# Identity transposes ahead of six matmul units of a perceiver block on one Trainium2 core

## The chip, the cores and the metric

The kernel runs on one core of a Trainium2 (trn2) chip. The metric is device time in microseconds (us) of one execution, the median of several runs. All data is float32.

## The reference

A block of a transformer over 32 sequences of 64 tokens, width 512, cut to what matters:

```python
x = x + cross_attention(layernorm(x), ctx, mask)   # 256 context tokens, one head, softmax
x = x + mla(layernorm(x))                          # 16 heads, low-rank q and kv, rope, causal
r = layernorm(x)                                   # FFN on 2048 tokens:
h = square(relu(r @ up_w))                         # 512 -> 2048
y = h @ down_w + (r @ expert_w) * top2(r @ gate_w).sum()
out = x + (layernorm(y) * gamma + beta)
```

## The kernel before

Only the last parts bear on the change. The kernel goes through five stages, one after the other on TensorE (PE): cross-attention and projections, the heads of the latent attention (b_q, b_s, b_t, b_v), the output projection ("op", matmuls into tiles op), the way up (tiles up) and the way down (tiles dp). The last three are matrix products of 2048 tokens, done as a scheme of seven block products in place of eight: a unit takes a left operand of 7 combined blocks and a right operand of 7, and writes seven products into four PSUM banks (`banks`, line 167: four tiles p0 to p3 of 128 x 2 x 256 float32, one bank each). Product s goes to half s % 2 of bank s // 2, so that the second half of bank 3 stays unused. Every operand is split into a high and a low part in fp32r (`split`, line 138: ACT's cast makes the high part, line 141; DVE's subtraction the low part, line 143), and every product is three matmuls: high by high, low by high, high by low (lines 699, 701, 702 in `seven`; line 1115 in `up_seven`, which has two blocks of the contraction and six matmuls a product).

The way up has 4 column blocks b by 8 weight slots k = 32 units of 42 matmuls, each 128x128 by 128x256. The weights wh_up and wl_up are the stationary operand there, the activations xr the moving one. In the first unit of each b (n = 0) four products go ahead with all but the last part of xr. After a unit `combine` (lines 154 to 162) adds the products on ACT and DVE, ACT squares (1183, 1184), and POOL adds the left blocks for the way down (`sums`, 149). Banks are double buffered (pool f_psp): a unit writes the banks of the last but one.

The way down has 8 token blocks by 8 slots = 64 units of 21 matmuls; the activations hl are stationary, the weights wh_down and wl_down moving. A token block accumulates its eight units in one set of banks. Units 0 to 15 alternate between the blocks 2 and 3 by fives and threes, then units 16, 24, 32, 40, 48 and 56 each begin a block. For every unit SP loads a tile c or dcw, POOL adds its missing blocks where they weren't stored (tokens of the first and the last column block), and ACT and DVE split it into hl (`left`), three units ahead of PE. After a block's last unit, `d_out` adds the experts' part (1260, 1262), normalizes (1269, 1270, 1285; the reciprocal root is POOL's power, line 121) and stores.

Before the way up, the last part of the projection stage turns the normalized tokens with transposes against the identity (line 959, tiles ops), and multiplies with the expert and gate weights (`o_expert`, tiles cpe; ACT scales into mo, lines 995 and 996, and issues the store itself, line 997). In the attention stage, b_t turns the softmax in groups of four transposes (line 779, tiles pst<-ident,s).

A recording layer (tc) orders the instructions of every engine by program order and its own estimate of readiness; `after(ins)` (line 135) pins what follows behind an instruction on its engine. Tiles come from pools at fixed places in SBUF; pools called gap shift what comes behind them. By those, the stationary and the moving operand of every fp32r matmul in the ways up and down lie at 32 and 96 bytes modulo 128 (wh_up 32, xr 96; hl 96, wh_down 32); the identity lies at 32.

Of the kernel before, what the change touches and what calls it, by code (L numbers as in the profile page):

```python
# [9 lines left out]
FP = mybir.dt.float32  # L10
# [8 lines left out]
P = 128  # L19
# [37 lines left out]

BETA_AT = 60

READ_AHEAD, READ_FAR = 5, 9  # L60

WARM = 10
# [17 lines left out]
def perceiver_block(ctx: ExitStack, tc: tile.TileContext, x, mem, mask, wq_a, bq_a, qnw, wq_b, bq_b,  # L80
                    wkv_a, bkv_a, kvnw, wkv_b, wo, bo, gate, up, down, expert, gamma, beta, cs, out):
    nc = tc.nc

    def pool(name, bufs=1, **kw):
        return tc.tile_pool(name=name, bufs=bufs, reuse_waits="tile", **kw)

    def gap(p, n, nm):

        p.tile([P, n // 4], FP, tag=f"gap_{nm}", name=f"gap_{nm}")
# [12 lines left out]
    cp = ctx.enter_context(pool("const"))  # L102
    mhalf = cp.tile([P, 2], FP, name="mhalf")
    nc.gpsimd.memset(mhalf, -0.5)
    pid = ExitStack()
    ident = pid.enter_context(pool("ident")).tile([P, P], FP, name="ident")
    make_identity(nc, ident)

    pows, stats_of, rooted = [], {}, {}
# [25 lines left out]
    def after(ins):  # L135
        return tc.issue_after(ins.ins) if ins is not None else ExitStack()
# [28 lines left out]
    def banks(pool, nm):  # L165

        return [pool.tile([P, 2, TB], FP, tag=f"p{i}", name=f"{nm}_{i}") for i in range(4)]
# [10 lines left out]
    with ExitStack() as mla:  # L178
# [409 lines left out]
        with ExitStack() as pb:  # L588
# [4 lines left out]
            one = pb.enter_context(pool("b_one"))  # L593
# [70 lines left out]
            cps, ops, reads = {}, {}, []  # L664
# [18 lines left out]
            def left(u, room=None, pins=(None, None)):  # L683
# [5 lines left out]
                ops[u] = (h, l)  # L689
                return low  # L690

            def seven(ps, k, h, l, steps=None, part=(0, 7)):

                wh, wl = wts[k]
                for s, (a, b) in list(enumerate(SEVEN))[slice(*part)]:
                    last = k == ORDER[-1] and s in (1, 3, 5, 6)

                    with after(first if k == 0 and s in (1, 3, 5) else None):
                        first = nc.tensor.matmul(  # L699
                            ps[s // 2][:, s % 2], h[:, a], wh[:, b], start=(k == 0 and s % 2 == 0), stop=False)  # L700
                    nc.tensor.matmul(ps[s // 2][:, s % 2], l[:, a], wh[:, b], start=False, stop=False)  # L701
                    ins = nc.tensor.matmul(ps[s // 2][:, s % 2], h[:, a], wl[:, b], start=False, stop=last)  # L702
                    if last and steps:
                        next(steps)
                return ins
# [116 lines left out]
            for j in range(n):  # L822
                g, blk = units[j]
# [47 lines left out]
            pss = {0: banks(ps_p, "op0")}  # L871
# [131 lines left out]
    for u, (blk, k) in enumerate(out_units):  # L1003
# [7 lines left out]
        if u >= 2:  # L1011
# [8 lines left out]
            o, steps = o_steps(blk, pss[blk]) if k == ORDER[-1] else (None, None)  # L1020
            seven(pss[blk], k, *ops.pop(u), steps)
        if u in SLOT_AT:
            i = 3 + SLOT_AT.index(u)
# [10 lines left out]
        if u in TURN_AT:  # L1034
            i = TURN_AT.index(u)
# [14 lines left out]
        if u in MULT_AT:  # L1050
            i = MULT_AT.index(u)
# [45 lines left out]
    for _ in o_expert(NB - 1, *xT):  # L1097
        pass
    pc.close()
    pid.close()  # L1100


    ps_p = ctx.enter_context(pool("f_psp", 2, space=PSUM))
    fp = ctx.enter_context(pool("f_act", 3))
    with ExitStack() as pu:
        gap(pu.enter_context(pool("gap4")), 192, "x")
        xps = [pu.enter_context(pool(f"u_x{i}")) for i in range(4)]

        def up_seven(ps, k, b, n, steps):
            wh, wl = (t[:, 0:7].rearrange("p a (k f) -> p a k f", k=2) for t in wts[k])  # L1110

            def product(s, parts, first=False, last=False):
                i, j = SEVEN[s]
                for m, (kk, w, low) in enumerate(parts):
                    nc.tensor.matmul(  # L1115
                        ps[s // 2][:, s % 2], w[:, i, kk], xr[b, 2 * kk + low][:, j],
                        start=(first and m == 0), stop=(last and m == len(parts) - 1),
                    )

            most = [(0, wh, 0), (0, wl, 0), (0, wh, 1), (1, wh, 0), (1, wl, 0)]  # L1120
            rest = [(1, wh, 1)]
            one, two = (0, 2, 4, 6), (1, 3, 5)
            late = None
            if n == 0:
                for s in one:
                    product(s, most, first=True)
            if n == 7:
                for s in one:
                    product(s, rest, first=True)
                for s in (0, 2, 4):  # L1130
                    product(s, most, last=True)
                for s in two:
                    product(s, rest, first=True)
                if b + 1 < NB // 2:
                    late = right(b + 1, 3)
            for s in range(7):
                if n == 0 and s in one:
                    product(s, rest, last=True)
                elif n < 7:
                    product(s, most + rest, True, True)  # L1140
                elif s in two or s == 6:
                    product(s, most, last=True)
                if s in (1, 3, 5, 6):
                    with after(late if s == 3 else None):
                        next(steps)
# [13 lines left out]
        for b in range(NB // 2):  # L1159
            if b == NB // 2 - 1:  # L1160
                first = [(blk, k) for ks in (ORDER[:5], ORDER[5:]) for blk in DOWN[:2] for k in ks]
# [3 lines left out]
            for n, k in enumerate(ORDER):  # L1165
# [11 lines left out]
                ps = banks(ps_p, f"up{b}_{k}")  # L1177
# [42 lines left out]
    with ExitStack() as pd:  # L1220
# [1 line left out]
        gab = wp.tile([P, D], FP, name="gab")  # L1222
        junk = wp.tile([P, D], FP, name="junk")
        sp = pd.enter_context(pool("d_small", 4))
        gap(pd.enter_context(pool("gap9")), 64, "hlq")
        hlq = pd.enter_context(pool("d_hl"))
        dcp = pd.enter_context(pool("d_c"))
        ap = pd.enter_context(pool("d_act", 2))
# [67 lines left out]
        def step(d, pins):  # L1296
            try:
                return d.send(pins)
            except StopIteration:
                return False  # L1300

        pss, xms, outs, read = {}, {}, [], 5
        for u, (blk, k) in enumerate(out_units):
            if k == ORDER[0]:
                pss[blk] = banks(ps_p, f"dp{blk}")
            while read <= min(max(u + READ_AHEAD, 2 * u + 1), u + READ_FAR, last_unit):
                read_pair(read, from_h, room_for(read))
                read += 1
            if u + 3 <= last_unit:
                room = hlq.tile([P, 7, TB], FR, tag="hl", name=f"hl{u + 3}") if u % 4 == 0 else None  # L1310
                low = left(u + 3, room=room)
            else:
                low = None, None
            o, steps = d_steps(blk, pss[blk]) if k == ORDER[-1] else (None, None)
            seven(pss[blk], k, *ops.pop(u), steps)
            if u in (8, 10) or (u > 15 and k == ORDER[4]):
                b = DOWN[(u - 8) // 2] if u < 16 else blk
                xms[b] = d_load(b)
            if u in (1, 4) and stores:
                store_h(*stores.pop(0))  # L1320
            if u == 6:
                nc.sync.dma_start(gab, gamma.partition_broadcast(P))
            if u in (1, 3, 5):
                put_slot(ORDER[5 + u // 2], "down", cs.pop(0))
            if u == 1:
                cs.append(read_slot(ORDER[7], "down"))
            outs = [d for d in outs if step(d, low)]
            if k == ORDER[-1]:
                outs.append(d_out(blk, o, *xms.pop(blk)))
                next(outs[-1])  # L1330
# [49 lines left out]
```

## Time and profile before

| what | value |
|---|---|
| runs | 1110.8, 1107.37, 1110.25 us; median 1110.25 |
| the profiled execution's own time | 1113.25 us |
| its span in the trace | 1111.5 us |
| mean granted TensorE clock | 0.989 |
| PE matmul busy | 1073.6 us, 97% |
| PE weight loads busy | 989.1 us, 89% |
| DVE, ACT, POOL busy | 773.3, 546.7, 509.3 us |
| way up, PE | from 781.19 to 939.8 us |
| way down, PE | from 940.56 to 1101.3 us |

How to read it: an execution is taken by the profiler, so its time stands beside the others, not among them. Busy time of PE is no measure of its pace, since matmuls overlap (one of 276 ns starts every 113 ns); the starts of matmuls in the timeline are. The granted clock is the share of full speed that the throttle let PE have. The chain of waits is followed back from the last instruction, at each step to what released it.

### The profile page before, as it was taken

Reading aid. Unit: us, or ns where it says so; the run is one execution under the profiler, and the core shown is the slowest. Engines: PE = TensorE matmul, PEld = TensorE weight load, DVE = VectorE, ACT = ScalarE, POOL = GpSimd, SP = SyncE. Lnnn points to the kernel's source line nnn. Section 1 sums busy time; section 2 is a strip of 40 time slices with the busy share of each in tenths; the row PEclk is TensorE's granted clock in tenths of the full one; section 3 lists DMA queues with packets and bytes.
Section 4 is the critical chain, followed back from the end, with each engine's and each line's share of the span. In section 5 each row is a group of like instructions: output and inputs, shape, how many; then the busy total and the mean of one; then the engine's idle time right before and its main releaser. Section 6 shows DMA issues by size and latency. Waiting matters only on the chain.

```text
span 1111.5 us, 25983 instructions
## 1 busy us (share of the span) xinstructions
PE 1073.6 (97%) x10182; PEld 989.1 (89%) x10182; DVE 773.3 (70%) x1363; ACT 546.7 (49%) x1048; POOL 509.3 (46%) x694
## 2 busy tenths in 40 slices
PE   8899999999999999999998999998999999999896
PEld 6677777689999999999888999998999999999896
DVE  4666666656766667666868866668776578698786
ACT  4444444433444434433555544445675667565543
POOL 3333333326778777774571200002058770056761
PEclk9999999999999999999999999999999999999998
DMA  8777666343686787773497776776766789998681
GB/s 266 224 230 234 212 209 207 110 159 125 252 276 212 249 273 274 257 244 109 146 367 277 254 229 229 218 284 239 239 190 201 236 290 280 307 314 253 188 247 58
DMA packets 195386, 254.67 MB, mean 229 GB/s; under 512 B 18544, under 2 KB 140032, under 8 KB 195264
## 3 DMA queue, kind: packets, MB, share of 16 engines
q1 hardware_dynamic: 190848, 241.45, 66.4%
q10 hardware_dynamic: 3456, 8.39, 2.1%
q0 software_dynamic: 960, 3.18, 0.8%
q8 instruction: 80, 1.31, 0.5%
q14 instruction: 42, 0.34, 0.1%
HBM read 146.67 MB, written 106.30 MB: 228 GB/s over the span
## 4 chain that ended last, share of the span: by engine, by line
PE 58%; DMA 13%; DVE 10%; POOL 6%; issue 5%; ACT 4%; SPq 2%; DVEq 0%; ACTq 0%; POOLq 0%
PE up L1115 9%; PE pss L749 6%; PE psq L173 4%; PE psq L174 4%; PE psq L175 4%; PE psv L793 3%; PE op L702 3%; PE op L701 3%; PE op L699 2%; DVE hl L143 2%; PE pse L173 2%; PE pse L175 2%; PE pse L174 2%; PE dp L701 2%; PE dp L702 2%
## 5 line engine op out<-in xcount | busy, mean ns | idle before, releaser
L731 DVE SCALAR_TENSOR_TENSOR qe<-pse,bqp,cq 64x256 f32<-64x256 f32 x256 | 123.7, 483 | 79.4 <-PE pse L175 73.5
L1115 PE MATMUL up<-xr,wh_up 128*128 128x256 f32 x896 | 156.7, 280 | 1.9 <-ACT up L154 1.9
L1115 PEld LDWEIGHTS up<-xr,wh_up 128*128 128x128 f32 x896 | 137.2, 190 | 2.3 <-ACT up L154 2.0
L701 PE MATMUL dp<-wh_down,hl 128*128 128x256 f32 x448 | 125.4, 280 | 4.2 <-DVE hl L143 4.2
L701 PE MATMUL op<-wh_wo,hl 128*128 128x256 f32 x448 | 125.9, 281 | 3.6 <-DVE hl L143 3.5
L143 DVE TENSOR_TENSOR hl<-c,hl 128x896 fp32r<-128x896 f32 x85 | 97.6, 1151 | 45.4 <-ACT hl L141 41.5
L699 PE MATMUL op<-wh_wo,hl 128*128 128x256 f32 x448 | 126.0, 282 | 1.8 <-ACT hl L141 1.8
L699 PE MATMUL dp<-wh_down,hl 128*128 128x256 f32 x448 | 125.2, 279 | 0.6 <-DVE uo L159 0.6
L702 PE MATMUL dp<-wl_down,hl 128*128 128x256 f32 x448 | 125.1, 279 | 0.0
L702 PE MATMUL op<-wl_wo,hl 128*128 128x256 f32 x448 | 124.9, 280 | 0.0
L1115 PE MATMUL up<-xr,wl_up 128*128 128x256 f32 x448 | 123.5, 279 | 0.0
L141 ACT CAST hl<-c 128x896 fp32r<-128x896 f32 x85 | 79.9, 941 | 80.7 <-PE op L702 33.1
L173 PE MATMUL psq<-qa_hi,qh 128*128 128x256 f32 x384 | 112.8, 294 | 0.0
L174 PE MATMUL psq<-qa_hi,ql 128*128 128x256 f32 x384 | 106.6, 278 | 0.0
L175 PE MATMUL psq<-qa_lo,qh 128*128 128x256 f32 x384 | 106.5, 277 | 0.0
L701 PEld LDWEIGHTS op<-wh_wo,hl 128*128 128x128 f32 x448 | 85.2, 190 | 5.1 <-DVE hl L143 5.0
L701 PEld LDWEIGHTS dp<-wh_down,hl 128*128 128x128 f32 x448 | 84.8, 189 | 4.6 <-DVE hl L143 4.6
L699 PEld LDWEIGHTS op<-wh_wo,hl 128*128 128x128 f32 x448 | 85.0, 190 | 2.7 <-ACT hl L141 2.0
L702 PEld LDWEIGHTS dp<-wl_down,hl 128*128 128x128 f32 x448 | 85.5, 191 | 0.0
L699 PEld LDWEIGHTS dp<-wh_down,hl 128*128 128x128 f32 x448 | 84.8, 189 | 0.7 <-issue 0.7
L702 PEld LDWEIGHTS op<-wl_wo,hl 128*128 128x128 f32 x448 | 84.8, 190 | 0.2 <-DVE wl_wo L143 0.2
L1115 PEld LDWEIGHTS up<-xr,wl_up 128*128 128x128 f32 x448 | 85.0, 190 | 0.0
(227 smaller groups left out, 3151.8 us busy)
## 6 DMA issues: line engine op xcount, KB each, us to landing
c<-vd SPq DMA_DIRECT2D x58, 448.0 KB, 4.2
cx<-in_ctx SPq DMA_DIRECT2D x32, 512.0 KB, 4.5
vd<-vw SPq DMA_DIRECT2D x29, 512.0 KB, 4.0
hd<-uo SPq DMA_DIRECT2D x107, 128.0 KB, 3.1
hd<-uw SPq DMA_DIRECT2D x21, 512.0 KB, 3.0
dcw<-hd SPq DMA_DIRECT2D x18, 448.0 KB, 5.5
vd<-v SPq DMA_DIRECT2D x30, 256.0 KB, 3.4
c<-hd SPq DMA_DIRECT2D x17, 448.0 KB, 6.2
```

Of the source, the lines that this page charges most:

```text
L141: copy = nc.scalar.copy(hi, src)
L143: return copy, engine.tensor_tensor(lo, src, hi.bitcast(FP), ALU.subtract)
L173: nc.tensor.matmul(ps, ah, bh, start=(j == 0), stop=False)
L174: nc.tensor.matmul(ps, al, bh, start=False, stop=False)
L175: nc.tensor.matmul(ps, ah, bl, start=False, stop=(j == n - 1))
L699: first = nc.tensor.matmul(ps[s // 2][:, s % 2], h[:, a], wh[:, b], start=(k == 0 and s % 2 == 0), stop=False)
L701: nc.tensor.matmul(ps[s // 2][:, s % 2], l[:, a], wh[:, b], start=False, stop=False)
L702: ins = nc.tensor.matmul(ps[s // 2][:, s % 2], h[:, a], wl[:, b], start=False, stop=last)
L731: rope = nc.vector.scalar_tensor_tensor(qe[64 * a : 64 * a + 64, :], pe[r, :], bqp[r, p : p + 1], cq[r, a, :], ALU.add, ALU.mult,)
L749: nc.tensor.matmul(ps[64 * j : 64 * j + 64, pj, b, :], qs[2 * pj + j][a][:, sl], kT[:, a, kt], start=(a == 0), stop=(a == 1),)
L793: nc.tensor.matmul(o, kv[a, i, :], t[a, bp, :], start=True, stop=True)
L1115: nc.tensor.matmul(ps[s // 2][:, s % 2], w[:, i, kk], xr[b, 2 * kk + low][:, j], start=(first and m == 0), stop=(last and m == len(parts) ...
```

## The change

Ahead of six units PE turns a 128x128 tile of the unit's stationary operand against an identity, twice, into the unused half of bank 3; nothing reads the result. The six are the first units of b = 0 and b = 2 of the way up, with wh_up against a second identity at 96 bytes modulo 128, which ACT copies from the first as the way up begins; and units 5, 16, 32 and 48 of the way down, with hl against the first identity, which now is kept to the end. Each tile turned lies 64 bytes from its identity modulo 128. The unit's matmuls are pinned behind the transposes (in the way up, those of its first four products), and in the way down the transposes behind the unit before. The second identity's place takes that of a gap ahead of the tiles of xr, and a gap in the way down grows, so that the other operands keep their places modulo 128.

```diff
--- before.py
+++ after.py
@@ -57,6 +57,8 @@
 
 BETA_AT = 60
 
+SETTLE_AT = (5, 16, 32, 48)
+
 READ_AHEAD, READ_FAR = 5, 9
 
 WARM = 10
@@ -102,8 +104,7 @@
     cp = ctx.enter_context(pool("const"))
     mhalf = cp.tile([P, 2], FP, name="mhalf")
     nc.gpsimd.memset(mhalf, -0.5)
-    pid = ExitStack()
-    ident = pid.enter_context(pool("ident")).tile([P, P], FP, name="ident")
+    ident = ctx.enter_context(pool("ident")).tile([P, P], FP, name="ident")
     make_identity(nc, ident)
 
     pows, stats_of, rooted = [], {}, {}
@@ -689,6 +690,13 @@
                 ops[u] = (h, l)
                 return low
 
+            def settle(ps, sta, one, behind):
+
+                for i in range(2):
+                    with after(behind):
+                        behind = nc.tensor.transpose(ps[3][:, 1, 0:P], sta.bitcast(FP), one)
+                return behind
+
             def seven(ps, k, h, l, steps=None, part=(0, 7)):
 
                 wh, wl = wts[k]
@@ -1097,13 +1105,14 @@
     for _ in o_expert(NB - 1, *xT):
         pass
     pc.close()
-    pid.close()
 
 
     ps_p = ctx.enter_context(pool("f_psp", 2, space=PSUM))
+    gap(ctx.enter_context(pool("gap11")), 192, "ident2")
+    ident2 = ctx.enter_context(pool("ident2")).tile([P, P], FP, name="ident2")
+    nc.scalar.copy(ident2, ident)
     fp = ctx.enter_context(pool("f_act", 3))
     with ExitStack() as pu:
-        gap(pu.enter_context(pool("gap4")), 192, "x")
         xps = [pu.enter_context(pool(f"u_x{i}")) for i in range(4)]
 
         def up_seven(ps, k, b, n, steps):
@@ -1122,8 +1131,9 @@
             one, two = (0, 2, 4, 6), (1, 3, 5)
             late = None
             if n == 0:
-                for s in one:
-                    product(s, most, first=True)
+                with after(settle(ps, wh[:, 0, 0], ident2, None) if b in (0, 2) else None):
+                    for s in one:
+                        product(s, most, first=True)
             if n == 7:
                 for s in one:
                     product(s, rest, first=True)
@@ -1222,7 +1232,7 @@
         gab = wp.tile([P, D], FP, name="gab")
         junk = wp.tile([P, D], FP, name="junk")
         sp = pd.enter_context(pool("d_small", 4))
-        gap(pd.enter_context(pool("gap9")), 64, "hlq")
+        gap(pd.enter_context(pool("gap9")), 128, "hlq")
         hlq = pd.enter_context(pool("d_hl"))
         dcp = pd.enter_context(pool("d_c"))
         ap = pd.enter_context(pool("d_act", 2))
@@ -1312,7 +1322,10 @@
             else:
                 low = None, None
             o, steps = d_steps(blk, pss[blk]) if k == ORDER[-1] else (None, None)
-            seven(pss[blk], k, *ops.pop(u), steps)
+            h, l = ops.pop(u)
+            even = settle(pss[blk], h[:, 0], ident, ends) if u in SETTLE_AT else None
+            with after(even):
+                ends = seven(pss[blk], k, h, l, steps)
             if u in (8, 10) or (u > 15 and k == ORDER[4]):
                 b = DOWN[(u - 8) // 2] if u < 16 else blk
                 xms[b] = d_load(b)
```

Lines 957 and up of the changed kernel are those of the kernel before moved by 8 to 13; `settle` is at lines 693 to 698, and line 1115 becomes 1124.

## Prediction

> **What bounds the kernel now.** I read four views, in this order: the table by stretches of time (which engine is full in the two ways), the chain that ended last, PE's timeline around waits and transposes, and ACT's timeline where the way up begins. All times are us from the start of the span.
>
> The chain first, from its list in order of time (start, us, what):
>
> ```profile
> 781.36 38.26 PE up L1115 x336
> 819.63 62.19 PE up L1115 x546
> 882.50 1.98 DVE xr L1086
> ...
> 1037.55 1.26 POOL dcw L149 x3
> ...
> 1041.83 1.27 DVE hl L143
> ```
>
> From 781 to 882 the chain is matmuls and nothing else: PE sets the time there. From 882.5 to 1043.1 it holds DMAs, DVE, ACT and POOL, and hardly a matmul: there PE waits for others (2.0 us at 921.3, 0.7 at 939.8, 1.4 at 955.0, 3.2 at 1039.9). After 1043.1 it is PE again up to the last matmul at 1101.3, and then the last block's DVE work.
>
> PE itself has two speeds at full clock. The same matmul, the group of line 701, taken in 941 to 1039 and in 1047 to 1101 (columns after the bar: busy us, mean ns of one):
>
> ```profile
> L701 PE MATMUL dp<-wh_down,hl 128*128 128x256 f32 x285 | 78.8, 276 | 1.2 <-DVE hl L143 1.2
> ```
>
> ```profile
> L701 PE MATMUL dp<-wh_down,hl 128*128 128x256 f32 x154 | 43.3, 281 | 0.0
> ```
>
> Of the difference the starts tell more: unit 20 of the way down starts at 989.82 and unit 21 at 992.20, so 21 matmuls take 2.380 us, 113.3 ns a step; units 50 and 51 start at 1066.80 and 1069.27, 2.473 us, 117.8 ns a step. Call them quick and slow. A unit of the way up (42 steps) is 4.760 or 4.947. The speed holds until PE is interrupted. In this execution up units 0 (first half) and 21 to 31 were slow, up units 1 to 20 quick, down units 0 to 40 quick, 42 to 63 slow.
>
> What transposes do to it, from PE's timeline (start, us):
>
> ```profile
> 545.72 0.28 PE L173 MATMUL pse<-qa_hi,qh 128*128 128x256 f32 x1
> 545.84 0.28 PE L174 MATMUL pse<-qa_hi,ql 128*128 128x256 f32 x1
> 545.96 0.28 PE L175 MATMUL pse<-qa_lo,qh 128*128 128x256 f32 x1
> 546.08 0.60 PE L779 MATMUL pst<-ident,s 128*128 128x128 f32 x4
> 546.43 0.37 PE L173 MATMUL psq<-qa_hi,qh 128*128 128x256 f32 x1
> ...
> 547.55 0.28 PE L173 MATMUL psq<-qa_hi,qh 128*128 128x256 f32 x1
> 547.66 0.28 PE L174 MATMUL psq<-qa_hi,ql 128*128 128x256 f32 x1
> ```
>
> Steps of 0.118 before, 0.113 after. Thirty such groups of four (tile and identity 64 bytes apart modulo 128, as in the change) stand in the attention stage: all were followed by quick steps, three of them after slow ones (257.6, 267.6, 546.1), as was the group at 559.7 that came after a wait.
>
> **The change part by part.** *Price of one pair.* From 545.96 to 547.55 is 1.59 us with four transposes and ten steps in it; ten quick steps are 1.13, so the four cost 0.46. They start 0.109 apart; two fewer leave 0.24 us a pair.
>
> *Pair ahead of up unit 0.* It does more than transpose: in the built order its first matmul waits for ACT's copy into ident2, which stands on ACT behind the last scaling of the experts (L996) and behind the issue of their store (L997):
>
> ```profile
> 781.82 0.49 ACT L996 ACTIVATE mo<-cpe,gs 128x256 f32<-128x256 f32 x1
> 782.34 0.33 ACTq L997 DMA_DIRECT2D mod<-mo  x1
> 784.63 0.37 ACT L154 COPY up<-up 128x256 f32<-128x256 f32 x1 [2.32 <-PE up L1115]
> ```
>
> ```profile
> 781.19 0.28 PE L1115 MATMUL up<-xr,wh_up 128*128 128x256 f32 x1
> ```
>
> Before, PE went straight on at 781.19. Now the issue ends at 782.67, the copy starts at about 782.70 and takes 0.27 (the 128x128 copy of line 492, median 270 ns), and PE follows 0.05 later (as after ACT's copy at 922.97): 783.02. The transposes start 0.165 and 0.109 apart after a wait (group at 559.7), and the first step after them takes 0.20, not 0.11: the unit runs as from 783.38 and ends at 788.14. Before it ended at 786.13, having lost 0.18 to slow steps and a 0.08 wait at 783.55 for xr's last part, which DVE has ready at 783.47, no longer late. **+2.01 us**, all on the chain: PE has nothing else queued, and behind it wait ACT's copy of line 154, DVE's and POOL's sums. Bounds: +0.06 if the copy were hidden (0.24 less 0.18), and +2.9 more if the clock drops (rival 2). I take 2.01, since it is read from the rows at the place itself.
>
> *Pair ahead of up unit 16* (857.84): it was quick already; **+0.24** on the chain. Its new wait, DVE's last sum of unit 14, is a unit old.
>
> *Pairs ahead of down units 5, 16, 32:* quick already. PE's waits at 955.0 (1.4) and 1039.9 (3.2) end with DVE's hl, not with PE, and cover 0.24 and 0.48: **0**; without the cover +0.72.
>
> *Pair ahead of down unit 48* (1061.85): 16 slow units turn quick, 16 x (2.473 - 2.380) = 1.49, less 0.24: **-1.25**. DVE's and ACT's parts of hl are there 2.2 us or more ahead of PE in units 48 to 63, so nothing is late next; the DVE end (1101.4 on) moves with the last matmul.
>
> *Moved rows:* in the built order DVE scales two output blocks (L1285, 1.03 us) ahead of hl37 and hl53 instead of behind, and ACT swaps their casts with a square; hl37 and hl53 had 2.2 and 3.0 us to spare: 0. POOL and SP keep their order. The new places of tiles keep the 64 byte relation. 0.
>
> Sum: 2.01 + 0.24 + 0 - 1.25 = **+1.0 us** on 1113.25, the profiled execution's time (span 1111.5): 1114.25. By the median of the runs, 1110.25/1113.25 = 0.9973: **1111.3 us**.
>
> *Rules against rows.* The Trainium skill, "TensorE: Matmul & The Clock Gate", Part 4: PE-mode transpose, says that the clock gate does not count transposes as PE activity as it does matmuls; by that the pair at up unit 0 would lengthen the idle time there and make rival 2 the forecast (+3.9). The rows say otherwise: 619.64 to 623.05, with eight transposes in it, kept the full clock. The same page, section Back-to-back issue gap, has one warm step, N/2.4 + 2.5 ns, an estimate of 109 ns here, and no second one; by it every pair is pure cost and the sum 2.01 + 0.24 + 0.24 = +2.5. The trace shows 113.3 and 117.8.
>
> **The rivals.** *1. The tail gains nothing* (the pair leaves slow steps slow, or the runs compared have a quick tail): 1.0 + 1.49 = +2.5, 1112.7. For it: no pair of two is in the trace, only fours and eights. Against: every group of four worked, and slow steps followed all four half-clock stretches, the one at 1042.9 among them.
>
> *2. The idle time before up unit 0 halves the clock.* The clock drops for 3.41 us at a time, the drops are whole multiples of 3.413 us apart, and what counts is the stretch just before (columns: length, PE busy, ..., PEclk):
>
> ```profile
> 619.64:623.05 3.41, 2.09 (x17) 1.68 (x15) 3.34 (x7) 2.40 (x4) 0.00 (x0) 1.00 0.67 222
> 623.05:626.47 3.42, 3.40 (x26) 3.20 (x27) 3.42 (x7) 1.04 (x2) 0.00 (x0) 1.00 0.69 189
> ...
> 920.01:923.42 3.41, 1.56 (x14) 1.39 (x13) 2.94 (x5) 3.32 (x6) 0.00 (x0) 1.00 0.76 284
> 923.42:926.84 3.42, 3.42 (x16) 3.42 (x17) 2.90 (x6) 2.88 (x5) 0.00 (x0) 0.50 0.89 243
> ```
>
> PE busy 1.56 (and 1.62 at 585.5) was too little, 2.09 enough. The new wait, 781.36 to 783.02, leaves 1.75 in a stretch that holds it whole, between the two; most positions of the stretch cut it in two and leave more. Price: steps of 213.3 instead of 113.3 ns for 3.41 us, 1.6; then slow steps, as after every such drop, for some seven units at 0.187, 1.3. In all +3.9, 1114.1: slower by 0.35%. It decides once the wait leaves less than about 1.6 busy; each 0.1 us of longer wait makes it likelier.
>
> *3. Slow steps of 882 to 940 matter after all* and the pair at unit 16 prevents them: 11 x 0.187 = 2.05 less, and 1.6 more if PE's wait at 921 then keeps the clock: -1.05 to -2.65, 1109.2 to 1107.6. Against: they began at 881.6 with a short wait, five units past that pair, and the chain leaves PE there.
>
> *4. The copy is early* (ACT's scaling ends sooner than PE's last expert matmul allows in this trace): 1.0 - 1.95 = -0.95; with rival 3, -3.0 to -4.6, 1105.7 at best. That would be faster by 0.4%.
>
> **How the numbers follow.** Forecast 0.50; rival 1 0.18; rival 2 0.18 (in a quarter of it with rival 1, 1115.6); rival 3 0.08; rival 4 0.06. The three runs spread over 3.4 us, two half-clock drops' worth, which blurs every case by about 1.7. 0.3%, 3.3 us, is about what a measurement of this kernel can tell from no change. Slower by more than that: rival 2 and some of rival 1, 0.23. Faster: rival 4 with 3 and spread, 0.07. The rest, 0.70, is within. The range, 1108.6 to 1114.8, takes in rivals 1 and 2 and the slower half of rival 3.
>
> **What would show it.** PE idle about 1.7 us before line 1124's first matmul, ended by ACT's copy; steps of 0.113 in all of up unit 0; no change of speed at unit 16; PE's waits at down units 6 and 41 shorter by the pairs' price; 2.380 us a unit from 48 on. I am wrong if PE starts the way up within 0.5 us, if the pair leaves slow steps, or if the waits between 882 and 1043 shrink by more than 0.7 us in all.

## The result, and the profile after

The kernel with the transposes takes **1114.53 us** (median of 10 runs, 1111.99 to 1116.74); the kernel before took 1111.65 us (10 runs, 1107.37 to 1113.06) timed beside it. The ratio is **1.0029, 95% interval 1.0015 to 1.0043**: slower by about 3.2 us, where +1.0 was forecast. The profiled execution, one of the ten, took 1115.56 us (span 1113.8, granted clock 0.992).

Where the time went is read from PE's starts, stage by stage. Each column is one execution; the second execution of each kernel ("again") was profiled later.

| from PE's starts, us | before | before, again | after | after, again |
|---|---|---|---|---|
| last expert matmul to first matmul of the way up | 0.12 | 0.12 | 1.74 | 1.74 |
| way up (first matmul to first of the way down) | 159.37 | 160.48 | 162.34 | 162.31 |
| way down (first matmul to last) | 160.75 | 157.11 | 158.28 | 158.98 |
| sum | 320.23 | 317.70 | 322.36 | 323.03 |
| half-clock stretches of 3.41 us in the two ways | 2 | 0 | 0 | 1 |

By the means the gap gives +1.62, the way up +2.4 and the way down -0.3: +3.7 us in all, beside the 3.2 (1.7 to 4.8) of the timed runs. So there are two things to explain: the gap, which was forecast, and a longer way up, which was not. The split by stage is rough. The half-clock stretches (923.4 and 1042.9 in before, 925.6 in after, again), at the 1.6 us each that the prediction worked out, are in the sums and differ by execution. And what lies ahead of the change varies more than the change costs: the last expert matmul starts between 778.2 and 785.1 us in the eighteen executions profiled, which is why sums and not spans are compared here.

**The gap.** PE's timeline in the profile after, where the way up begins (start, us, what; in brackets the idle time and what ended it):

```profile
781.24 0.28 PE L176 MATMUL cpe<-we_lo,oh 128*128 128x256 f32 x1
782.78 0.44 PE L697 MATMUL up<-ident,wh_up 128*128 128x128 f32 x2 [1.26 <-ACT ident L1113]
782.98 0.36 PE L1124 MATMUL up<-xr,wh_up 128*128 128x256 f32 x1
```

and ACT's there:

```profile
781.56 0.47 ACT L1004 ACTIVATE mo<-cpe,gs 128x256 f32<-128x256 f32 x1
782.06 0.33 ACTq L1005 DMA_DIRECT2D mod<-mo  x1
782.43 0.30 ACT L1113 COPY ident<-ident 128x128 f32<-128x128 f32 x1 [0.40 <-ACT mo L1004]
```

Scaling, issue of the store, copy, and 0.05 later PE: the chain is the one that the prediction drew. ACT's last scaling began 0.32 after the last expert matmul's start here, 0.74 in the profile before (781.08 to 781.82), where ACT's cast of xr had ended late; so the wait is 1.26, not 1.66.

**The clock.** The stretch of 3.41 us just before the way up (columns: length, PE busy, PEld, DVE, ACT, POOL busy, granted clock, DMA share, GB/s):

```profile
779.60:783.01 3.41, 2.15 (x20) 1.95 (x18) 2.59 (x4) 2.66 (x6) 0.00 (x0) 1.00 0.63 197
783.01:786.42 3.41, 3.41 (x31) 3.41 (x30) 0.63 (x1) 0.00 (x0) 0.00 (x0) 1.00 0.96 341
```

With 2.15 busy the next stretch has the full clock: no half-clock drop, as the forecast had it.

**The pace.** The durations of the same matmul show it at a glance: 276 ns among quick steps (113.3 ns from start to start), 281 among slow steps (117.8). From 787 to 877 (units 1 to 19 of the way up in the kernel before, 0 to 18 in the kernel after; min/median/max ns, first and last start); first the kernel before:

```profile
L1115 PE MATMUL up<-xr,wh_up x529: 276/276/356, 786.8 to 876.9; 128*128 128x256 f32 x177
```

then the kernel after:

```profile
L1124 PE MATMUL up<-xr,wh_up x510: 281/281/364, 786.9 to 876.9; 128*128 128x256 f32 x170
```

PE was quick there and is slow now, up to unit 28. In the second executions the kernel before was quick in units 0 to 20 again; the kernel after was slow to unit 15 and quick from 16 on, yet its way up was as long: PE then waited 3.1 us ahead of unit 29 (at 925.3), where the first execution had waited 1.3, and a half-clock stretch followed. In the way down, the same view of the low by high matmul (line 709) in units 8 to 15 and 17 to 40:

```profile
L709 PE MATMUL dp<-wh_down,hl x54: 276/276/276, 964.7 to 982.8; 128*128 128x256 f32 x54
...
L709 PE MATMUL dp<-wh_down,hl x155: 281/281/281, 985.1 to 1039.7; 128*128 128x256 f32 x155
```

Units 42 to 47 are quick again (median 276) after the wait at 1046.3, 49 to 63 slow again (281). The two changes from quick to slow stand exactly at the pairs of units 16 and 48. PE's timeline at unit 16:

```profile
983.79 0.28 PE L709 MATMUL dp<-wh_down,hl 128*128 128x256 f32 x1
983.90 0.28 PE L710 MATMUL dp<-wl_down,hl 128*128 128x256 f32 x1
984.01 0.38 PE L697 MATMUL dp<-ident,hl 128*128 128x128 f32 x2
984.15 0.36 PE L707 MATMUL dp<-wh_down,hl 128*128 128x256 f32 x1
984.35 0.28 PE L709 MATMUL dp<-wh_down,hl 128*128 128x256 f32 x1
984.47 0.28 PE L710 MATMUL dp<-wl_down,hl 128*128 128x256 f32 x1
```

Steps of 0.11 up to the pair, 0.12 after it. From 983.90 to 984.35 the pair costs 0.45 less two quick steps, 0.22 us (0.24 was forecast); what it leaves behind is the opposite of what was forecast.

### The profile page after: what moved, and what is told of

Its sections match the earlier page's. It is cut to its first block, busy times and chain, and to the rows that moved or that the text cites. A ratio compares the mean times of both kernels' runs of the same rounds, so it can differ in the third digit from the quotient of the medians.

```text
span 1113.8 us, 26008 instructions
## 1 busy us (share of the span) xinstructions
PE 1076.4 (97%) x10194; PEld 990.4 (89%) x10194; DVE 772.6 (69%) x1363; ACT 547.2 (49%) x1049; POOL 506.2 (45%) x694
## 4 chain that ended last, share of the span: by engine, by line
PE 27%; DMA 8%; DVE 7%; ACT 3%; issue 2%; POOL 2%; SPq 1%; DVEq 0%; ACTq 0%; POOLq 0%
PE up L1124 11%; PE op L710 2%; PE op L709 2%; PE op L707 2%; DVE hl L144 2%; PE dp L709 2%; PE dp L710 2%; PE dp L707 2%; DMA cw_wo<-wd_wo 2%; DMA c<-hd 1%; DMA cw_down<-wd_down 1%; PE cpe L175 1%; PE cpe L174 1%; PE cpe L176 1%; DMA dcw<-hd 1%
## 5 line engine op out<-in xcount | busy, mean ns | idle before, releaser
L1124 PEld LDWEIGHTS up<-xr,wh_up 128*128 128x128 f32 x896 | 137.5, 189 | 2.4 <-ACT up L155 1.5
```

What stands on the lines that cost most here:

```text
L1124: nc.tensor.matmul(ps[s // 2][:, s % 2], w[:, i, kk], xr[b, 2 * kk + low][:, j], start=(first and m == 0), stop=(last and m == len(parts) ...
```

## The experiments

Three accounts are tested. *The wait*: the cost is PE's wait for ACT's copy, and the pairs are worth next to nothing. *The slow pair*, in two forms that stood when the first four kernels were written: the pairs leave PE slow, because two transposes are too few, or because of the place of the tiles and weights that they stand ahead of. *The draw*, which came with the kernel counts: the pairs do not set a pace; every interruption of PE, a pair as well as a wait, lets it come out quick or slow, and the changed kernel loses by the slow stretches behind them. Beside these, whether the 64 bytes matter.

The table holds all executions with a profile. Times are from PE's starts as above (gap: last expert matmul to first matmul of the way up); the pace is that of the way up's units, q quick, s slow, without odd units behind the waits at its end; the ratio is to the kernel before, timed beside it, and stands where a kernel was timed in several runs. Half-clock stretches lie in the two ways of before (2), after_again (1), up0_pool (2), six (2) and apart (1).

| kernel | gap | way up | way down | sum | pace of the way up | ratio, 95% interval |
|---|---|---|---|---|---|---|
| before | 0.12 | 159.37 | 160.75 | 320.2 | 0-20 q, 21-31 s | |
| before_again | 0.12 | 160.48 | 157.11 | 317.7 | 0-20 q, 21-29 s | |
| after | 1.74 | 162.34 | 158.28 | 322.4 | 0-28 s | 1.0029 [1.0015, 1.0043] |
| after_again | 1.74 | 162.31 | 158.98 | 323.0 | 0-15 s, 16-31 q | |
| pool_copy | 0.25 | 158.29 | 159.75 | 318.3 | 0-20 q, 21-28 s | 1.0007 [0.9986, 1.0027] |
| up_only | 1.73 | 160.07 | 158.98 | 320.8 | 0-15 q, 16-31 s | 1.0024 [1.0009, 1.0039] |
| up_only_again | 1.73 | 163.12 | 157.21 | 322.1 | 0-28 s | |
| down_only | 0.12 | 161.96 | 156.84 | 318.9 | 0-28 s | 0.9992 [0.9976, 1.0009] |
| four | 1.95 | 159.59 | 157.69 | 319.2 | 0-15 q, 16-30 s | 1.0012 [0.9992, 1.0032] |
| up0_only | 1.73 | 162.81 | 159.31 | 323.9 | 0-31 s | 1.0066 [1.0047, 1.0086] |
| up0_again | 1.73 | 162.44 | 156.97 | 321.1 | 0-28 s | |
| up16_pool | 0.12 | 161.24 | 159.12 | 320.5 | 0-15 s, 16-30 q | 1.0013 [0.9996, 1.0030] |
| up0_pool | 0.26 | 156.66 | 160.07 | 317.0 | 0-26 q, 27-28 s, 29-31 q | 1.0009 [0.9995, 1.0023] |
| up0_pool_again | 0.26 | 158.88 | 157.28 | 316.4 | 0-30 q | |
| six | 0.72 | 159.62 | 161.39 | 321.7 | 0-30 q | 1.0026 [1.0007, 1.0045] |
| six_again | 0.69 | 162.18 | 158.50 | 321.4 | 0-29 s | |
| counts | 0.12 | 170.18 | 158.33 | 328.6 | 19 of 32 q | |
| apart | 0.12 | 167.17 | 161.20 | 328.5 | 8 of 32 q | |

### Which part costs: pool_copy, up_only, down_only, four

**pool_copy** takes the wait away: POOL, idle there, makes the copy.

```diff
-    nc.scalar.copy(ident2, ident)
+    nc.gpsimd.tensor_copy(ident2, ident)
```

> The copy into ident2 is moved from ACT to POOL, which is idle then; nothing else changes. Both theories (the pairs leave PE slow because two transposes are too few; or because of the place of the tiles and weights they stand ahead of) expect the same here: PE's gap ahead of up unit 0, 1.53 us in the changed kernel, falls to 0.3 (bank 3 is still released by ACT's scaling of the experts, at about 781.5), so 1.2 to 1.4 us less than the changed kernel, a ratio to the kernel before of about 1.0017, with up units 0 to 20 still slow at 4.947. A rival, that the late start is the whole loss, expects 1.0003 or less.

Measured 1.0007 [0.9986, 1.0027]; the gap is 0.25 us. The transposes are all still there, and most of the loss is gone (the intervals of 1.0029 and 1.0007 overlap, so this alone does not settle it). The ratio lies between the two that were expected, and units 0 to 20, expected slow, were quick: a pair does not always leave slow steps.

**up_only** keeps the pairs of the way up alone:

```diff
-SETTLE_AT = (5, 16, 32, 48)
+SETTLE_AT = ()
```

> The two pairs of the way up alone; the four of the way down are left out. If the slow way up is the loss (21 units on the chain at 0.187, 3.9 us, and 1.6 for the late start, part of which later waits of PE take back), the ratio to the kernel before stays at that of the changed kernel, about 1.0025 (1.0015 to 1.0035). If the pairs of the way down carry the loss, it falls to 1.0005 or less.

Measured 1.0024 [1.0009, 1.0039], the loss of the whole change, as expected if the way up carries it. But in the profiled execution units 0 to 15 were not slow, so the profile does not show the reason that the expectation gave.

**down_only** keeps those of the way down alone, without the copy:

```diff
-    nc.scalar.copy(ident2, ident)
...
-                with after(settle(ps, wh[:, 0, 0], ident2, None) if b in (0, 2) else None):
+                with after(None):
```

> The four pairs of the way down alone, no second identity is written. If the slow way up is the loss, the ratio to the kernel before is 1.000 within 0.0010: units 16 to 41 turn slow, which PE's wait at unit 41 (3.2 us in the kernel before) covers, and units 48 to 63 are slow either way. If the pairs of the way down carry the loss, it is 1.002 or more.

Measured 0.9992 [0.9976, 1.0009]: the pairs of the way down neither cost nor bring anything that can be measured. The expected pace did not come: units 5 to 31 were quick, 32 to 40 slow, 42 to 63 quick. And its way up, without a pair, was slow in units 0 to 28 (161.96 us): the unchanged stream of matmuls is not always quick, and a slow way up alone did not make this execution's sum, 318.9, longer than the mean of the two of before, 319.0, since its way down was quick to the end.

**four** has four transposes in place of two:

```diff
-                for i in range(2):
+                for i in range(4):
```

> Four transposes in place of two at all six places. Theory one, that two are too few (all groups of four or eight in both traces were followed by quick steps): up units from 0 on and down units from 5, 16, 32 and 48 on run at 4.760 and 2.380, the time falls by 3.9 in the way up and rises by 6 x 0.22 at most, ratio to the kernel before 1.000 to 1.001. Theory two, that the place counts (all six stand ahead of slot 0, whose weights lie 512 bytes modulo 1024 from those of the slots ahead of which the groups of eight stood): the same units stay slow, 4.947 and 2.473, ratio 1.003 to 1.004.

Measured 1.0012 [0.9992, 1.0032]. Of its six groups four were followed by quick steps; of the 18 pairs in the traces of after, pool_copy, up_only and down_only it was seven. So a pair does not reliably leave PE quick, which was the step that the forecast rested on; nor do four, and the place alone does not leave it slow. The ratio lies between the two that were expected and decides nothing.

### What decides the pace: counts and apart

**counts** puts 1, 2, 3, 4, 6 or 8 transposes ahead of every unit of the way up (by b: 2 and 4 by turns, 4 and 2, 1 and 3, 8 and 6), and 2, 4, 8, 2, 4, 8 ahead of six units of the way down, with POOL's copy (in the traces of counts and apart the groups of units 0 and 1 stand inside the units, not ahead of them):

```diff
-            def settle(ps, sta, one, behind):
+            def settle(ps, sta, one, behind, n=2):
-                for i in range(2):
+                for i in range(n):
...
+            with after(settle(ps, wh[:, 0, 0], ident2, past[0], ((2, 4) * 4, (4, 2) * 4, (1, 3) * 4, (8, 6) * 4)[b][n])):
```

> A probe of PE's pace: ahead of each of the 32 units of the way up stand 1, 2, 3, 4, 6 or 8 transposes (2 and 4 ten times each... in blocks 0 and 1 by turns 2,4 and 4,2; 1 and 3 in block 2; 8 and 6 in block 3), and ahead of six down units 2, 4, 8, 2, 4, 8. All results stay as they are; the copy into ident2 is on POOL, so that no unit waits for ACT. Read is the step after each group, 113 ns (quick) or 118 ns (slow). Theory one, the number decides: groups of 8 and 4 are followed by quick steps 9 times in 10 or more, pairs 2 times in 10 or fewer. Theory two, the place decides (what comes directly before and after the group): all counts share one outcome, as after the same wait. Theory three, each interruption draws the pace anew, by the phase it falls in: every count comes out both ways, between 3 and 7 times in 10. The time itself says little (some 110 transposes at about 0.11 us and what the pace gives).

Measured, quick steps behind so many of the groups (ways up and down together): 1 transpose 1 of 4, 2: 4 of 10, 3: 3 of 4, 4: 7 of 10, 6: 4 of 4, 8: 5 of 6. Neither of the pure cases: groups of four and more were quick 16 times in 20, not 9 in 10, and no count but six had one outcome. What came before the group matters as well. Two groups of the way down break into the same undisturbed quick stream, the last gap before the first transpose 115 ns in both: the eight at 1031.68 and the two at 1051.61. The view of durations behind the one and behind the other, up to the next group:

```profile
L709 PE MATMUL dp<-wh_down,hl x55: 276/276/276, 1033.0 to 1051.4; 128*128 128x256 f32 x55
...
L709 PE MATMUL dp<-wh_down,hl x54: 281/281/281, 1051.9 to 1070.7; 128*128 128x256 f32 x54
```

Behind the eight 276 ns, quick; behind the two 281, slow. This holds without exception over all eighteen traces: a pair that broke into quick steps with a last gap of 114 or 115 ns was followed by slow steps 11 times of 11, a group of four, six or eight by quick steps 13 times of 13. Where the last gap was 117 ns or more, or the steps before were slow, pairs came out both ways (25 of 59 quick), as they did behind a wait (3 of 9). The rule was read off the traces; all but two of its 24 cases were in hand when it was first written down, in the expectation of six.

**apart** puts a pair ahead of every unit of the way up, by turns from the identity 64 bytes from the tile and from the one at the same place modulo 128, the rest as in counts:

```diff
+            with after(settle(ps, wh[:, 0, 0], (ident2, ident)[(n + b) % 2], past[0], 2)):
```

> A probe of the 64 bytes: ahead of each of the 32 units of the way up stand two transposes, by turns from the identity that lies 64 bytes from the transposed tile (modulo 128) and from the one that lies at the same place modulo 128; ahead of six down units pairs as in the change. The copy into ident2 is on POOL. If the 64 bytes matter, the units behind the 64-byte pairs are quick 8 times in 10 or more and the others 3 times in 10 or fewer. If each interruption draws the pace anew, the two kinds differ by no more than 3 of 16.

Measured: behind the pairs 64 bytes apart 2 of 16 quick, behind those 0 bytes apart 6 of 16, and 4 of 6 in the way down (64 bytes). The difference of 4 in 16 is larger than the draw account allowed and against the 64 bytes; with such numbers it can be chance. That 64 bytes make a pair leave quick steps 8 times in 10 is refuted.

### The wait and the pace apart: up0_only, up16_pool, up0_pool, six

**up0_only** has the pair ahead of up unit 0 alone, with ACT's copy:

```diff
-SETTLE_AT = (5, 16, 32, 48)
+SETTLE_AT = ()
-                with after(settle(ps, wh[:, 0, 0], ident2, None) if b in (0, 2) else None):
+                with after(settle(ps, wh[:, 0, 0], ident2, None) if b == 0 else None):
```

> Only the pair ahead of up unit 0 is left, with ACT's copy; no other pair. If the wait for ACT's copy is what costs, PE is idle 1.3 to 1.7 us ahead of line 1124's first matmul and the ratio is 1.001 to 1.0025. If the pace behind the pair of unit 16 is what cost, the ratio is within 0.0005 of 1.

Measured 1.0066 [1.0047, 1.0086], about 7 us: far more than either case. The wait is the same (1.3 us idle, the gap 1.73), so the rest is something else. The same view as above, 787 to 877:

```profile
L1124 PE MATMUL up<-xr,wh_up x512: 281/281/281, 786.7 to 876.8; 128*128 128x256 f32 x171
```

All 32 units are slow. So were 29 in the profile of down_only, whose timed runs lost nothing: that slow units make up the rest of the 7 us is not shown.

**up16_pool** has the pair ahead of unit 16 alone, with POOL's copy (b == 2 in the line above).

> Only the pair ahead of up unit 16 is left, its identity copied on POOL, so no unit waits for the copy. If the wait is what cost, the ratio is 0.9995 to 1.001 (two transposes are 0.24 us, 0.0002). If the pair draws a slow pace for units 16 to 31 out of a quick one and that reaches the end, up to 16 x 0.187 = 3.0 us or 1.0027; but the waits between 882 and 943 stand behind those units and cover part.

Measured 1.0013 [0.9996, 1.0030]: nothing that the measurement can tell from no change. This way up was slow to unit 15 with no pair ahead of it, and turned quick at the pair.

**up0_pool** is up0_only with POOL's copy.

> Only the pair ahead of up unit 0, its identity copied on POOL, so that PE does not wait for ACT's copy. The kernel with ACT's copy was 1.0066 [1.0047, 1.0086]. If the wait for the copy (1.6 us of PE) is all its cost, the ratio is 0.9995 to 1.0010 now. If the pace behind the pair is the rest (up to 32 x 0.187 = 6.0 us, less what the waits from 921 to 943 cover), the ratio is 1.003 to 1.005 where units 0 to 31 are slow in the profile, and about 1.000 where they are quick.

Measured 1.0009 [0.9995, 1.0023], and the way up quick. PE's timeline, where no wait is left:

```profile
780.84 0.28 PE L176 MATMUL cpe<-we_lo,oh 128*128 128x256 f32 x1
780.96 0.38 PE L697 MATMUL up<-ident,wh_up 128*128 128x128 f32 x2
```

and 787 to 877:

```profile
L1124 PE MATMUL up<-xr,wh_up x531: 276/276/276, 786.9 to 877.0; 128*128 128x256 f32 x177
```

The two kernels differ in who makes the copy and in nothing else, and the intervals of their ratios, each to the kernel before timed beside it, do not overlap. By the profiles (two executions of each) the sums are 322.5 and 316.7: 1.5 of the gap, 4.9 of the way up (162.6 and 157.8), -0.5 of the way down. So ACT's copy costs more than the wait for it; that the rest is the pace behind the wait is what these four profiles show, slow in both of the one kernel, quick in both of the other, and not the timed runs, whose paces are not known.

**six** puts six transposes ahead of up unit 0 and of down unit 48, with POOL's copy (range(6), SETTLE_AT = (48,), b == 0).

> Six transposes in place of two, ahead of up unit 0 and down unit 48 alone, identity copied on POOL. In the profiles so far groups of 4, 6 and 8 that break into undisturbed quick steps (the gap before the first transpose 115 ns) were followed by quick steps 12 times in 12, pairs 0 times in 9. If the number sets the phase, up unit 0 on and down unit 48 to the end are quick in the profile, and the ratio is 0.998 to 1.0005 (twelve transposes are 1.3 us, the waits cover none of the last six). If each interruption is a draw that the number does not sway, a stretch is slow and the ratio is 1.000 to 1.003.

Measured 1.0026 [1.0007, 1.0045], although the profile shows quick steps behind both groups. Quick steps do not bring what they seem to, for one because the way up has a second limit. The chain of waits of six (start, us, what):

```profile
912.44 8.35 DMA cw_down<-wd_down
920.81 1.05 ACT wh_down L142
```

and PE's timeline ahead of unit 29:

```profile
924.79 0.36 PE L1124 MATMUL up<-xr,wh_up 128*128 128x256 f32 x1 [3.26 <-ACT up L155]
```

ACT's timeline shows what its sum (line 155) stands behind, and SP's when the load was issued:

```profile
920.81 1.05 ACT L142 CAST wh_down<-cw_down 128x1024 fp32r<-128x1024 f32 x1 [3.49 <-DMA cw_down<-wd_down]
...
924.38 0.36 ACT L155 COPY up<-up 128x256 f32<-128x256 f32 x1
```

```profile
907.60 3.10 SPq L1158 DMA_DIRECT2D hd<-uo  x1
...
911.88 0.44 SPq L1164 DMA_DIRECT2D hd<-uw  x1
912.44 0.77 SPq L641 DMA_DIRECT2D cw_down<-wd_down  x1
```

ACT and DVE, whose sums free the banks for unit 29, stand behind the cast of a weight slot for the way down, and this behind its load, which lands at 920.81, 137.6 us after the way up began. PE reached that place 138.0 us after its start (921.26), where the kernel before was at 140.1, and waited 3.4 (from the starts, less a step) where that had waited 2.0. Both had a half-clock stretch there, six at 925.1 and before at 923.4, and another in the way down. The load isn't free of PE either: SP issues it, at 912.44, behind stores of the sums (hd). In the chain of the kernel after,

```profile
916.00 8.16 DMA cw_down<-wd_down
924.18 1.06 ACT wh_down L142
```

it lands 141.2 after the start of the way up (783.0), in that of the kernel before 138.2 (919.39 less 781.19). Slow ways up (up0_only and up0_again 140.8 both, six_again 141.1) are so 3 to 5 us later at this place than quick ones (136.0 and 137.5 in up0_pool's two, 137.6 in six), of the 29 x 0.187 = 5.4 that the steps alone would give. How the 2.9 us of six's timed runs come about is not shown: its two profiled executions had sums of 321.7, with two half-clock stretches, and 321.4, with a slow way up (below).

### The same programs again: before_again, up0_again, after_again, up_only_again, up0_pool_again, six_again

Each is the kernel of its name, unedited, in a second execution.

> The unchanged kernel in another execution: do the paces of its way up and way down come out as in the first profile? If an interruption's outcome is fixed by the program, up units 1 to 20 are quick and 21 on slow again, down units to 41 quick and 42 on slow. If each execution draws anew, at least one of these four stretches has the other pace.

The way up came out as in the first profile (quick to unit 20, slow from 21), the way down did not: quick to the end, where units 42 to 63 had been slow.

> The kernel with only the pair ahead of up unit 0 (ACT's copy) in another execution. If the slow pace of all 32 up units behind it belongs to the program, they are slow again, and the time is above 1114. If it was one draw, some 15 units or more are quick.

Slow again, units 0 to 28; 1116.97 us.

> The changed kernel in a second execution. If the pace behind the pair and the wait belongs to the program, up units 0 to 28 are slow again, and from the last expert matmul to the last matmul of the way down it takes 322.4 us within 1. If each execution draws it, there is about an even chance of quick units behind unit 0 and 319 to 321 us.

Units 0 to 15 slow again, but the pair of unit 16, which had left slow steps slow, now turned them quick; in the way down units 33 to 40 were quick behind the pair of unit 32, and slow in the first execution. The sum was 323.0, as before within 1.

> The kernel with the pairs of the way up alone, in a second execution. If the pace belongs to the program, units 0 to 15 are quick and 16 to 31 slow again. If each execution draws it, at least one of the two halves is likely to have the other pace.

Units 0 to 28 slow where 0 to 15 had been quick: behind the same wait and the same pair, in the same program. The view of durations, first execution and second:

```profile
L1124 PE MATMUL up<-xr,wh_up x403: 276/276/276, 788.9 to 857.0; 128*128 128x256 f32 x135
...
L1124 PE MATMUL up<-xr,wh_up x387: 281/281/281, 788.8 to 856.9; 128*128 128x256 f32 x194
```

> The pair ahead of up unit 0 alone, identity copied on POOL, in a second execution. Without a wait for ACT the pair breaks into the same stream of expert matmuls each time: if the pace behind a pair without a wait belongs to the program, units 0 to 27 are quick again and the way up takes 156.7 us within 1.

Quick again, and 158.88 us, out of the "156.7 within 1": the load landed 137.5 after the start and PE waited 3.3 us ahead of unit 29, the wait that the next expectation puts at unit 28.

> Six transposes ahead of up unit 0 and down unit 48, in a second execution: quick again behind both. If a quicker way up only waits longer, PE's wait at unit 28 is 3 us or more again, and the way up takes 159 to 160 us as in the unchanged kernel, whose last 11 units were slow. If that wait and the half-clock stretch behind it were chance, the way up takes 157 to 158 us.

Not quick again: units 0 to 29 slow behind the same six transposes, 162.18 us. Behind the six ahead of down unit 48 they were quick. So a program does not own a pace: the same interruption leaves quick steps in one execution and slow steps in another. The case found in counts, a group that breaks into undisturbed quick steps, is the one exception seen.

## Why the prediction was wrong, step by step

- **Price of one pair, 0.24:** right, 0.22.
- **Up unit 0, +2.01:** the mechanism was right (PE waits for the copy, which stands behind scaling and issue on ACT); as to size, the wait was 1.26 and not 1.66, because ACT's cast of xr had ended earlier, and the start of the way up is 1.62 later.
- **"The first step after them ... the unit runs as from 783.38", quick, and a slow half unit regained:** wrong. Behind the wait and the pair PE was slow in unit 0 of after, after_again, up0_only, up0_again and up_only_again, quick in up_only. That is the step that failed: the state behind the interruption was taken from the groups of four and put at quick, and the way up came out 2.4 us longer by the means of two executions each. Rival 1 (the pair leaves slow steps) was priced for the tail alone, 1.49, and not for the way up. That the slow steps are what made the timed runs longer is argued from these profiles, not shown by itself.
- **Up unit 16, "it was quick already", +0.24:** the stream was slow when it got there; the pair left it slow once and turned it quick once.
- **Down units 5, 16, 32 at 0:** right in the sum, for down_only is 0.9992 [0.9976, 1.0009]; not in the pace, which turned slow at unit 16. The wait at 1039.9, 3.2 before, was 0.6 after (1046.3): it took up most of the lateness, slow units and all, as it was to take up two transposes. By the prediction's own sign of being wrong (waits between 882 and 1043 shorter by more than 0.7 in all) this counts too: those over 0.2 us, from 882 to 1047, add up to 7.7 before and 4.6 after.
- **Down unit 48, -1.25:** the gain did not come. The stream was quick there, at 1063.9, and the pair turned it slow; in after_again it was slow and the pair left it slow; before_again shows that the unchanged tail is quick in some executions, so there were no 1.49 us to win for certain.
- **The evidence:** thirty groups of four, all followed by quick steps, were read as "a pair sets PE quick". In each of the eighteen traces 31 of the 32 groups of the attention stage were followed by quick steps (the last, at 553.4 in the kernel before, by two matmuls and a wait), so the rows were read rightly. The steps from four to two and from that stage to the ways up and down were not in them: in the ways, groups of four left quick steps 11 times of 16 (counts and four), and pairs break the pace 11 times of 11 in just the undisturbed quick stream that the forecast counted on.
- **Moved rows, 0:** no run took them alone; down_only, which has those of the way down, shows no loss.
- **Rivals:** 1 had the mechanism, too small (+2.5) for the reason above; by the number rival 2 (+3.9) is as near to +3.2. 2 did not happen: 2.15 us busy kept the clock. Nor do slow steps follow every half-clock stretch, as its price had it: in after_again and six quick ones followed those at 925.6 and 925.1. Its doubt about transposes can be read from the kernel before: of the 28 matmuls from 199.79 to 203.21 25 are transposes, and the stretch behind it had the full clock. 3 did not: the waits between 882 and 943 went on (1.4 at 926.6, 1.7 at 943.5). 4 did not: the copy was late in all seven executions that had it on ACT (after, up_only, up0_only, each twice, and four).

The Trainium skill, "TensorE: Matmul & The Clock Gate", section Back-to-back issue gap, by which each pair is pure cost with no gain to follow, was weighed against the rows and set aside; its sum of +2.5 lay closer to the measured 3.2 than the forecast. The page gives that formula for an isolated matmul, and its figures for streams with weight loads are for other widths than 256. It has no second pace; both steps, 113.3 and 117.8 ns, are in every trace of this case.

What stays open: what decides between quick and slow (the last gap of 114 to 115 ns marks one case in which it is fixed; no run shows what it is); whether the wait (1.54 us from start to start) as such favours slow steps (five of six behind wait and pair, none of three behind the same pair without the wait: pool_copy and up0_pool twice), since six draws are few and no kernel has the wait without transposes; and why up0_only is 1.0066 and up_only 1.0024 (the intervals do not overlap), while the profiles of the two, 323.9 and 321.1 beside 320.8 and 322.1, do not part so clearly, and up0_only was timed in six runs only. A pair at unit 16 that can end a slow stretch would fit, but that is only argued. No version was measurably faster than the kernel before.

## What to carry to other kernels

Evidence that a group of four operations leaves an engine in a good state says little of a group of two, or of four in another stage: cost the state behind an interruption both ways, and over every stretch behind it, not only where you hope for the gain. An instruction that resets something is not free of its operands: ask which engine makes them and what is queued ahead of that, and let an idle engine do it (in pool_copy POOL's copy took 2.15 us and ended 2.1 us before PE's transposes). And before crediting a quicker stream, look for the next limit on it: here a weight load 138 us on took back part of every gain.

## What the runs showed of the hardware

- The stream of fp32r matmuls of 128x128 by 128x256, each with a weight load, has two stable paces at full clock, 113.3 and 117.8 ns a step (276 and 281 ns long in the records), and keeps one for up to 100 us and more; pairs of transposes and waits can change it.
- In an undisturbed quick stream (last gap 114 or 115 ns) the outcome went by the number: 2 transposes slow (11 of 11), 4, 6 or 8 quick (13 of 13); 1 and 3 were slow (2 and 1 cases).
- The same program draws differently in two executions (up_only: units 0 to 15 quick in one, slow in the other), and the sum of gap and ways differs by only 1.3 us (320.8 and 322.1): the way up was 3.05 us longer, the way down 1.77 shorter, since it was quick from unit 42 to the end in the second execution and slow from unit 46 in the first.
- What the clock does next goes by PE's busy time in the stretch of 3.41 us before, with a narrow doubtful band: over the eighteen traces the busiest stretch followed by half clock had 1.71 us (pool_copy, from 580.44) and the least busy one followed by full clock 1.59 (up0_pool_again, from 922.12).
